# Moving the output projection and the first half of the values within a turn of a pre-norm transformer kernel

## Chip, cores, metric

The kernel runs on one core of one Trainium2 chip. The metric is the device time of one execution in microseconds; less is better. The kernel before takes 3188.39 us (median of 3 runs, 3187.64 to 3191.98).

## What is computed

The input is 16 sequences of 256 tokens of 128 channels, float32. First comes one windowed attention with 16 heads of 8 channels, then six layers, each of an attention and a gated feed-forward. The change lies in the six layers' attention alone:

```python
# x is shifted by one token in half its channels; 16 heads of 64, windows of 32 tokens
q, k, v = split(x @ Wqkv)                  # 128 -> 3 * 1024
q, k = rotary(l2norm(q) * qs), rotary(l2norm(k) * ks)
sim = einsum('bhwie,bhwje->bhwij', q, look(k)) * 8      # own window and the one before
attn = softmax(where(mask, -max, sim))
out = einsum('bhwij,bhwje->bhwie', attn, look(v))
x = out.reshape(b, n, 1024) @ Wo + x
```

## The kernel before

**Tiles and turns.** A layer's 4096 tokens are cut in 32 tiles of 128 tokens. Six layers make 192 tiles, and the main loop (from L904) runs one turn per tile, with a few turns more at the end. A tile passes through several turns: in turn t the kernel projects tile t (`stage_p`), turns round K and Q of tile t-1 and scores it (`stage_s`), takes the exponentials of tile t-2 (`stage_e`), multiplies the probabilities of tile t-3 with its values (`stage_v`), projects the output of tile t-5 (`stage_w`), and does a part of the feed-forward of an earlier pair of sequences (`stage_f`), which is spread over four turns.

**The order inside a turn.** Every stage is a generator. `merge_at` (L248) sorts the steps of all stages by a number between 0 and 1 that the tables of L27 to L29 give them, ties by the order of the stages in the list, and runs them in that order. `mul` and `flip` (L290, L293) pin each TensorE instruction behind the one before, so this order is TensorE's order to the letter. The other engines' orders are made by the framework's scheduler from the same emission; each engine takes its own queue strictly in order, and a PSUM buffer is handed on when its last reader is done.

**The steps of a turn.** These names are used throughout:

- P0 to P5: the six projections of `project` (L626; places c/6): K in two halves, Q in two halves, V in two halves. Each is three matmuls of 128x512 with four 128x128 transposes of `turned` (L610) between them: K halves of tile t-1 in P0 and P1, Q halves in P2 and P3, the probabilities of tile t-2 in P4 and P5. After P0 to P3, DVE multiplies by the rotary table (`mc`, L644), ACT squares (`sq`, L653), DVE reduces the square (`r`, L654), POOL adds the products (`sum`, L655); after the second half of K or Q, ACT takes Ln and Exp of `r` (L659, L660, listed as L275), and POOL clamps `r` (L661) and scales (L665). After P4 and P5, ACT copies `vb` (L671). The transposes are copied by ACT (`kt`, `qt` L622; `pt` L620).
- E: `stage_e`, two matmuls that add the negated maxima to the scores; ACT then takes the two exponentials `p` (L758, listed as L275).
- VA and VB: the first and the second half of `stage_v` (places 0.1 and 0.45). Each is 32 small matmuls into two banks. DVE takes reciprocals and multiplies (`rc` L792, `of` L793), ACT rounds (`ohl` L797), POOL subtracts (`ohl` L798); after VB one DMA transposes `ohl` into `ot` (L801).
- W: `stage_w` (place 0.47), 24 matmuls of `ot` with the output weights; DVE adds the result to the residual (`xg`, L819, two instructions).
- S: `stage_s` (place 0.72), two mask matmuls and 128 small score matmuls; DVE takes the maxima (`nm`, L740).
- Feed-forward, by the turn's number modulo 4: kind 0 centres at 0.86 (FC; ACT squares, L858); kind 1 takes the statistics at 0.06 (ST; ACT Ln and Exp, DVE L864, ACT L867, DVE L868) and two gate projections at 0.74 and 0.88; kind 2 has the third gate projection at 0.03 and two of the other projections at 0.27 and 0.8 (DVE L888); kind 3 the last of these at 0.1 and the second weight matrix at 0.35 (W2; DVE L897, two instructions). The three Gelus on ACT (L281) need their own table, loaded before the first and changed back after the last.

**PSUM.** Eight banks in three pools: two banks for the projections, four shared by transposes, W, VA and the feed-forward, two shared by the scores and VB (`SPLIT`, `USE`, `USE_V`). So VB can start only when the exponentials have read the scores (VB's first bank after the first exponential, the second after the second), and S only when DVE's multiplications `of` have read VB's two banks. W of tile t-5 reads the `ot` that was transposed two turns before.

Of the kernel before, what the change touches and what calls it, by code (L numbers as in the profile page):

```python
# [24 lines left out]
KT = 2  # L25
LAG_S, LAG_P, LAG_V, LAG_W = 1, 2, 3, 5
AT_P = tuple(c / 6 for c in range(6))  # L27
AT_E, AT_V, AT_W, AT_S = (0.2, 0.21), (0.1, 0.45), (0.47,), (0.72,)
AT_F = ((0.86,), (0.06, 0.74, 0.88), (0.03, 0.27, 0.8), (0.1, 0.35, 0.6))  # L29
AT_L = 0.71  # L30
LOAD_AT = 6
# [992 lines left out]
```

## Time and profile before

The profiled execution took 3188.3 us; its span is 3186.5 us, and 1.8 us lie around it. The granted TensorE clock was 0.984 of full speed on average. Busy shares of the span: TensorE matmul 93%, weight load 65%, DVE 80%, ACT 75%, POOL 79%.

The windows view shows where the time lies: 250.0 us to 3140.0 us is the main loop, with 2772.2 us of TensorE, 2349.6 us of DVE, 2167.8 us of ACT and 2355.6 us of POOL busy in 2890 us.

The timeline gives the start of every step on TensorE. This table has the median time from the start of a step to the start of the next, over the 45 or 46 whole turns of each kind. A step takes longer than in other kinds where it, or the first instruction of the next step, waits.

| kind | steps and us from start to start, in TensorE's order | whole turn, median (mean) |
|---|---|---|
| 0 | P0 1.18, VA 0.80, P1 1.09, E 0.43, P2 1.18, VB 1.00, W 1.35, P3 1.08, P4 1.18, S 1.74, P5 1.09, FC 0.86 | 13.06 (13.28) |
| 1 | P0 1.08, ST 0.97, VA 0.79, P1 1.09, E 0.43, P2 1.62, VB 1.26, W 1.35, P3 1.08, P4 1.18, S 1.70, gate 0.66, P5 1.08, gate 0.65 | 14.99 (15.24) |
| 2 | P0 1.45, gate 1.27, VA 1.43, P1 1.09, E 0.43, proj. 0.65, P2 1.45, VB 1.26, W 1.35, P3 1.08, P4 1.18, S 1.74, proj. 0.66, P5 1.08 | 16.14 (16.21) |
| 3 | P0 1.18, VA 1.06, proj. 0.66, P1 1.08, E 0.43, P2 1.08, W2 2.67, VB 0.79, W 1.35, P3 1.08, P4 1.18, S 1.70, P5 1.09 | 15.46 (15.56) |

Four turns are 59.65 us by the medians and 60.29 us by the means. About half of the turns also prepare a piece of the next layer's weights (place 0.71), which adds an instruction or two on ACT and DVE and lengthens the means.

### The profile page before, as it was taken

The numbers are of one execution on the slowest core, as the hardware profiler recorded it, in microseconds if no ns is written. First come the engines' busy times: TensorE is split into PE (matmuls) and PEld (weight loads), VectorE is DVE, ScalarE is ACT, GpSimd is POOL, SyncE is SP. The second block draws the span as 40 slices with busy tenths as digits, with TensorE's granted clock in tenths as the row PEclk, the third lists the DMA queues.
The fourth block names the chain that finished last, engine by engine and source line by source line (L and its number), as shares of the span: only waits on it lengthen the run. The fifth ranks groups of instructions, "written<-read, shape, count | busy, mean of one in ns | idle before, by whom it ended". The sixth has DMA issues, their size and how long they took to land. (4 is left out here: it accounts for less than half of the span.)

```text
span 3186.5 us, 153142 instructions
## 1 busy us (share of the span) xinstructions
PE 2973.4 (93%) x67106; PEld 2081.1 (65%) x67106; DVE 2558.8 (80%) x4690; ACT 2378.3 (75%) x4970; POOL 2525.0 (79%) x2594
## 2 busy tenths in 40 slices
PE   4778999999999999999999999999999999999997
PEld 3555766666666666666666666666666666666664
DVE  6887888888788887788888788888788888878874
ACT  7877777777777777777777777777777777777774
POOL 6767988778888788888788888888888888887882
PEclk9958999999999999999999999999999999999999
DMA  5773444444344434444444444444344444344443
GB/s 118 143 132 81 102 103 94 87 93 88 85 108 100 86 85 94 89 96 103 90 89 82 93 101 99 87 89 92 84 103 106 85 87 96 83 92 106 91 88 72
DMA packets 622942, 302.96 MB, mean 95 GB/s; under 512 B 533446, under 2 KB 545732, under 8 KB 622276
## 3 DMA queue, kind: packets, MB, share of 16 engines
q1 hardware_dynamic: 622276, 293.18, 43.6%
q8 instruction: 528, 8.65, 1.1%
q14 instruction: 138, 1.13, 0.1%
HBM read 22.45 MB, written 4.19 MB: 8 GB/s over the span
## 5 line engine op out<-in xcount | busy, mean ns | idle before, releaser
L291 PE MATMUL bank<-wqkv,xhl 128*128 128x512 f16 x3456 | 1236.6, 381 | 7.7 <-ACT sq L653 6.3
L655 POOL TENSOR_TENSOR sum<-mc 128x512 f32<-128x512 f32 x768 | 994.7, 1298 | 234.1 <-DVE mc L644 223.2
L644 DVE TENSOR_TENSOR mc<-bank,tq 128x1024 f32<-128x1024 f32 x768 | 928.0, 1218 | 147.1 <-PE bank L294 136.3
L665 POOL TENSOR_TENSOR sum<-sum,r 128x512 f32<-128x512 f32 x768 | 795.6, 1057 | 31.9
L654 DVE TENSOR_REDUCE r<-sq 128x8 f32<-128x512 f32 x768 | 520.4, 682 | 276.3 <-ACT sq L653 266.4
L294 PE MATMUL bank<-ident,sum 128*128 128x128 f32 x3072 | 711.3, 273 | 0.7 <-POOL sum L665 0.7
L798 POOL TENSOR_TENSOR ohl<-of,ohl 128x512 f16<-128x512 f32 x384 | 451.1, 1175 | 210.8 <-ACT ohl L797 210.1
L653 ACT ACTIVATE sq<-bank 128x512 f32<-128x512 f32 x768 | 459.4, 608 | 161.8 <-DVE mc L644 160.4
L294 PEld LDWEIGHTS bank<-ident,sum 128*128 128x128 f32 x3072 | 433.1, 141 | 134.2 <-issue 17.5
L291 PEld LDWEIGHTS <-xhl 128*128 128x128 f16 x3456 | 338.0, 98 | 187.4 <-issue 16.7
L797 ACT CAST ohl<-of 128x512 f16<-128x512 f32 x384 | 237.8, 619 | 271.2 <-DVE of L793 268.4
L291 PE MATMUL bank<-vb,pt 64*32 64x65 f32 x6144 | 377.0, 225 | 50.3 <-ACT p L275 26.2
L291 PEld LDWEIGHTS bank<-vb,pt 64*32 64x32 f32 x6144 | 257.4, 105 | 218.5 <-ACT p L275 74.3
L294 PE MATMUL bank<-ident,p 128*128 128x128 f32 x1536 | 354.6, 273 | 0.0
L291 PE MATMUL bank<-v,pt 64*32 64x65 f32 x6144 | 313.5, 224 | 38.5 <-ACT p L275 17.7
L291 PE MATMUL bank<-vw,pt 64*32 64x65 f32 x12288 | 332.4, 225 | 1.8 <-issue 1.5
L793 DVE TENSOR_TENSOR of<-bank,rc 128x256 f32<-128x256 f32 x768 | 295.4, 416 | 1.8
L291 PE MATMUL bank<-ot,wohl 128*128 128x128 f16 x4608 | 291.3, 220 | 0.4 <-DMA ot<-ohl 0.4
L291 PEld LDWEIGHTS bank<-kt,qt 64*32 64x32 f32 x24576 | 256.3, 105 | 44.7 <-issue 44.2
L291 PE MATMUL bank<-kt,qt 64*32 64x64 f32 (+1 forms) x24576 | 284.7, 223 | 0.7 <-issue 0.7
L291 PEld LDWEIGHTS bank<-v,pt 64*32 64x32 f32 x6144 | 235.6, 105 | 70.1 <-ACT p L275 33.1
L291 PEld LDWEIGHTS <-wohl 128*128 128x128 f16 x4608 | 258.9, 98 | 19.1 <-issue 1.3
(155 smaller groups left out, 4965.6 us busy)
## 6 DMA issues: line engine op xcount, KB each, us to landing
v<-vb SPq DMA_DIRECT2D x384, 130.0 KB
vw<-vb SPq DMA_DIRECT2D x384, 130.0 KB
vw<-vb SPq DMA_DIRECT2D x576, 65.0 KB
wraw<-in_L_ffn_Wqkv_dram SPq DMA_DIRECT2D x36, 256.0 KB
wraw<-in_L_ffn_Wo_dram SPq DMA_DIRECT2D x12, 256.0 KB
ot<-ohl SPq DMA_TRANSPOSE x192
xt<-in_L_attn_x_dram SPq DMA_DIRECT2D x8, 256.0 KB
r1d<-xt SPq DMA_DIRECT2D x8, 256.0 KB
```

The lines of the kernel that those rows point to most:

```text
L291: pin(T.matmul(*args, **how))
L294: pin(T.transpose(*args))
L644: V.tensor_tensor(prod, p4.unsqueeze(3).to_broadcast([128, 8, 2, 2, 32]), tq[:, s, d.j].unsqueeze(1).to_broadcast([128, 8, 2, 2, 32]), ALU ...
L653: S.activation(sq, pp.rearrange("p (h d) -> p h d", d=64), AF.Square)
L654: V.tensor_reduce(r[:, hb * 8 : hb * 8 + 8], sq, AX.X, ALU.add)
L655: G.tensor_tensor(mc, m2[:, :, 0], m2[:, :, 1], ALU.add)
L665: G.tensor_tensor(mc, mc, rb.unsqueeze(2).to_broadcast([128, 8, 64]), ALU.mult)
L793: V.tensor_tensor(of[:, :, a], po[a][:, :, 0:64], rc.unsqueeze(2).to_broadcast([128, 4, 64]), ALU.mult)
L797: S.copy(ohl[:, 0, h], of)
L798: G.tensor_tensor(ohl[:, 1, h], of, ohl[:, 0, h], ALU.subtract)
```

## The change

Two numbers of the table of places change:

```diff
-AT_E, AT_V, AT_W, AT_S = (0.2, 0.21), (0.1, 0.45), (0.47,), (0.72,)
+AT_E, AT_V, AT_W, AT_S = (0.2, 0.21), (0.18, 0.47), (0.44,), (0.72,)
```

VA moves from 0.1 to 0.18, and so from behind P0 to behind P1 (P1 stands at 0.167); in kind 3 it also falls behind the feed-forward's projection at 0.1, with which it was tied. W moves from 0.47 to 0.44 and VB from 0.45 to 0.47, so W stands in front of VB. TensorE's order of a turn without feed-forward was P0, VA, P1, E, P2, VB, W, P3, P4, S, P5, and is P0, P1, VA, E, P2, W, VB, P3, P4, S, P5. No instruction is added or removed, and the SP queue keeps its order apart from single transposes that change place with a small load or store.

The other engines' orders follow in the built program. On DVE, kind 0 as an example (the numbers of P in brackets):

```
before: mc(0) rc rc of(VA) r(0) of(VA) mc(1) mc(2) r(1) rc rc r(2) of of(VB) xg xg(W) mc(3) r(3) nm nm
after:  mc(0) mc(1) r(0) rc rc r(1) of of(VA) mc(2) xg xg(W) r(2) rc rc of of(VB) mc(3) r(3) nm nm
```

In each kind `mc(1)` now stands in front of VA's normalization and the two `xg` in front of VB's. On ACT, `kt` of P1 and `sq` of P1 come in front of the exponentials, and behind VB's `ohl` come, as before, `vb` of P4, `pt` of P4 and `sq` of P3, then Ln and Exp, `vb` of P5, `pt` of P5 and, in kind 0, the square of FC. `qt` of P3 stood behind VB's `ohl` in all kinds; it now stands in front of it in kinds 1 and 2.

## The prediction

> **What bounds the kernel now.** I read the page first, then the view of waits, then the timeline engine by engine over four turns without weight pieces: P0 starts at 1241.03 us (kind 3), 1256.14 (kind 0), 1269.12 (kind 1) and 1284.11 (kind 2), and the four turns repeat after 59.21 us.
>
> ```profile
> span 3186.5 us, 153142 instructions
> PE 2973.4 (93%) x67106; PEld 2081.1 (65%) x67106; DVE 2558.8 (80%) x4690; ACT 2378.3 (75%) x4970; POOL 2525.0 (79%) x2594
> ```
>
> TensorE is almost always busy on the page, but a row ends by model, so a wait shorter than the 0.2 us that a small matmul lasts is hidden in it. The table of starts shows more: VB loses 0.10 + 0.21 us in kind 0 (the P2 in front of it takes 1.18 where 1.08 is free, VB 1.00 where 0.79 is), 0.54 + 0.47 in kind 1, 0.37 + 0.47 in kind 2 and nothing in kind 3. That is 2.16 us in four turns. The waits and TensorE's timeline in kind 1 say for what:
>
> ```profile
> ACT ohl L797 <- DVE of L793: 268.4, 238, 2.5
> DVE r L654 <- ACT sq L653: 266.4, 338, 2.2
> ACT r L275 <- DVE r L654: 150.8, 205, 1.9
> PE bank L291 <- ACT p L275: 43.9, 166, 2.9
> ```
>
> ```profile
> 1275.14 0.30 PE L291 MATMUL bank<-vb,pt 64*32 64x65 f32 x2 [0.40 <-ACT p L275]
> 1275.62 0.24 PE L291 MATMUL bank<-v,pt 64*32 64x65 f32 x1 [0.19 <-ACT p L275]
> ```
>
> VB waits for both exponentials. The first three rows show the other loop: ACT stands idle until DVE has normalized (`of`), DVE until ACT has squared, ACT until DVE has reduced. DVE's and ACT's timelines at the end of the turn of kind 0:
>
> ```profile
> 1263.11 0.24 DVE L792 RECIPROCAL rc<-bank 128x4 f32<-128x4 f32 x2
> 1263.28 0.69 DVE L654 TENSOR_REDUCE r<-sq 128x8 f32<-128x512 f32 x1
> 1263.88 0.75 DVE L793 TENSOR_TENSOR of<-bank,rc 128x256 f32<-128x256 f32 x2
> 1264.54 0.58 DVE L819 SCALAR_TENSOR_TENSOR xg<-bank,xg 64x128 f32<-64x128 f32 x2
> 1265.15 1.23 DVE L644 TENSOR_TENSOR mc<-bank,tq 128x1024 f32<-128x1024 f32 x1
> ```
>
> ```profile
> 1264.66 0.62 ACT L797 CAST ohl<-of 128x512 f16<-128x512 f32 x1 [0.82 <-DVE of L793]
> 1265.19 0.58 ACT L622 COPY qt<-bank 128x512 f32<-128x512 f32 x1
> 1265.66 0.59 ACT L671 COPY vb<-bank 128x512 f32<-128x512 f32 x1
> 1266.14 0.60 ACT L620 COPY pt<-bank 128x512 f32<-128x512 f32 x1
> 1266.62 0.62 ACT L653 ACTIVATE sq<-bank 128x512 f32<-128x512 f32 x1
> 1268.05 0.31 ACT L275 ACTIVATE r<-r,tiny 128x16 f32<-128x16 f32 x1 [0.81 <-DVE r L654]
> 1268.39 0.22 ACT L275 ACTIVATE r<-r 128x16 f32<-128x16 f32 x1
> 1268.51 0.57 ACT L671 COPY vb<-bank 128x512 f32<-128x512 f32 x1
> 1268.97 0.59 ACT L620 COPY pt<-bank 128x512 f32<-128x512 f32 x1
> 1269.45 0.61 ACT L858 ACTIVATE gt<-bank 128x512 f32<-128x512 f32 x1
> ```
>
> The reader is to see that DVE goes from row to row without a pause, and that nine ACT instructions stand in file behind VB's `ohl`. The last is FC's square, done at 1270.06; ST, which waits for it, starts on TensorE at 1270.21, directly behind P0 (1.08 after 1269.12). This file has about 0.1 us to spare. In turns with weight pieces it has none: P0 of kind 1 takes 1.31 in the mean against 1.08.
>
> **The change part by part.** Nothing is added or removed, DMAs included; the `ot` that W reads was transposed two turns earlier, so W in front of VB waits for no transfer, and VB's own transpose, later on SP, is read two turns on (some 28 us). Every price below is a row's start to the next start: `mc` 1.13 us (1.22 to its end), `r` 0.60, `rc` 0.08, `of` 0.33, the two `xg` 0.61, an ACT copy or square of 512 columns 0.48 to 0.50 (0.60 to its end), and 1.25 from a P's start to its `mc` (1257.39 after 1256.14).
>
> *W in front of VB: the wait goes.* W's 1.35 us of TensorE lie between P2 and VB and cover 0.31, 1.01 and 0.84: by itself 2.16 us in four turns. The main loop holds 46 such groups, so 99 us. The cover holds although `sq` of P1 now stands in front of the exponentials on ACT: in kind 0 the second exponential ends at 1261.36 instead of 1260.98, and VB starts at 1262.15.
>
> The Trainium skill would stop here: Perfetto Trace Analysis, section Optimization Strategy, has one find the gaps on the most contended engine and make what they wait for start sooner or finish faster. By that rule alone the sum is 3188 less 99, 3089 us; the rows of DVE and ACT speak against it.
>
> *What is late next, kind 0.* DVE has the same work up to `mc(3)`, but the two `xg` now precede VB's normalization. From `mc(1)` at 1258.52: mc, r, 2 rc, r, 2 of, mc, 2 xg, r, 2 rc, 2 of with the pause of 0.2 between `rc` and `of`, end 1265.28 instead of 1264.63: 0.65 later, the two `xg`. `mc(3)` stays (1265.19 for 1265.15). S, at 1265.20, just misses waiting. But `ohl` starts at 1265.32 instead of 1264.66, and the file behind it shifts: `sq(3)` 1267.27 for 1266.62, FC's square to its end 1270.69 for 1270.06, ST 1270.74 for 1270.21. TensorE, 0.07 ahead at P5, now waits 0.6 there: 0.53 lost.
>
> *Kind 1.* ST is 0.53 late, P1 follows it (VA no longer stands between), `mc(1)` at 1272.94. From there DVE has no pause: mc, r, L864 0.62, 2 rc, r, 2 of, mc, L868 0.60, 2 xg, r, 2 rc, 2 of end at 1280.68. VB's 1.01 is won and given back: P4 waits 0.35 for `sq(2)`, S some 0.6 for `of`. S starts, its second mask matmul counted, at 1280.52 instead of 1280.02: still 0.5 late. `sq(3)` is 0.65 late, and with it Ln, Exp, the table load and the three Gelus.
>
> *Kind 2* hangs on those Gelus. VA behind P1 hides part of its 1.26 us of waiting (for `pt` of P5 and the second Gelu), but P2 then waits for `sq(0)` behind the second table load and its transposes for `kt` (0.65 + 0.26). VB's 0.84 is won; DVE, which now waits for `sq(0)` before VA's reciprocals, brings `of(VB)` to 1297.37. S at 1297.20 for 1296.76: 0.44 late, 0.06 won back.
>
> *Kind 3* had no wait at VB, W2 covered it. S comes 12.20 after P0 instead of 12.31, but `of(VB)` ends 0.75 later (1252.88 for 1252.13 on the sample's clock), `sq(3)` 0.64 and `vb` of P5 0.6 later.
>
> *Kind 0 again.* P1 stands directly behind P0 and needs the bank that `vb` of P5 frees: 0.38 of waiting, where VA covered it before. P2 starts 59.91 us after P2 four turns earlier, against 59.21: **0.70 us lost in four turns**.
>
> POOL has the same 12 us a turn; K's scaling comes earlier since `r` of P1 does, so I cost it at nothing. Its cover is 2890 less 2356 us idle, 2.8 us a turn; were that gone, a `sum` of 1.27 would stand in the file.
>
> The skill's page SBUF — State Buffer, section SBUF: two separate sides, says a DVE instruction with two SBUF inputs and a POOL instruction that reads SBUF exclude each other. The trace agrees: the `sum` at 1275.81, beside L868, took 1.65 us against a mean of 1.30. At 0.35 us for each of the 46 L868, 16 us would fall on POOL, whose idle time takes it up.
>
> Sum: 46 times 0.70 is 32 us. Against the profiled execution: 3186.5 + 32 + 1.8 around the span = 3220; its own 3188.3 is the median of 3188.39. **Forecast 3220 us.**
>
> Bounds. Weight pieces add 50 DVE instructions L137 of 0.6 us (ten pieces in each of five layers). I take them at nothing more than before, because most keep their place between VB's `of` and `mc(3)`; all on the path would be 30 us, 3250. The other end is the first rival's.
>
> **The rivals.**
>
> A, faster. ACT's file ends 0.65 later but nobody waits: then kind 0 keeps 0.17 (0.31 less a wait of P2 for `sq(0)`), kind 1 nothing, kind 2 0.40, kind 3 0.10, together 0.67 in four turns, 31 us: 3157. It decides if `of(VB)` is under 0.1 us late in kind 0, as it is if DVE reaches the `xg` before VB's matmuls are done. For it: ACT idles 25% of the span. Against it: DVE's rows show no pause there.
>
> B, no change: waits only move, since DVE sets the pace in both orders (`mc(3)` at the same time in kinds 0 and 1): 3188. For it: those equal times. Against it: ACT's file is longer than DVE's lead.
>
> C, clearly slower: weight pieces lengthen both files, as P0 of kind 1 shows (0.23 in the mean): 3250. Against it: the pieces already cost that before.
>
> **How the numbers follow.** Forecast 0.58 (3197 to 3240), A 0.22, B 0.11, C 0.09. What a measurement tells from no change is 0.2%, 6 us. Faster takes A and a little of B: 0.24; the same most of B: 0.09; slower the rest: 0.67. Range 3152 to 3258: from a little beyond A to a little beyond C.
>
> **What would show it.** Right: no group of VB with `ACT p` as releaser on TensorE; VB's `of` 0.6 or more later against S; new waits of ST for L858, of P1 in kind 0 for `vb`, of P4 for `sq`, of S for `of`; whole turns of kinds 0 and 1 longer by 0.2 to 0.6 each. Wrong: ST starting directly behind P0 in turns without weight pieces, or four turns under 59.2 us.

## The result

The changed kernel takes 3280.38 us (median of 5 runs, 3279.14 to 3283.08) against 3188.14 us before (5 runs beside it, 3185.98 to 3191.98): 1.0289 times as long, 95% interval 1.0275 to 1.0303, or 92 us more. The direction was as forecast, the size not: 32 us were forecast, and the time lies outside the range.

The page of the changed kernel:

```profile
span 3281.3 us, 152963 instructions
PE 2998.9 (91%) x67106; PEld 2075.6 (63%) x67106; DVE 2631.2 (80%) x4690; ACT 2350.1 (72%) x4970; POOL 2525.8 (77%) x2594
```

DVE runs the same 4690 instructions and is busy for 72 us longer (2631.2 against 2558.8). TensorE's busy time rises by 26 us, which I take for waits that fall inside rows of modelled length. So the first question is which DVE instructions became longer. The second is what TensorE now waits for (total us, times, longest):

```profile
ACT ohl L797 <- DVE of L793: 405.3, 190, 3.9
DVE r L654 <- ACT sq L653: 295.5, 370, 1.5
ACT r L275 <- DVE r L654: 143.1, 174, 1.1
PE bank L291 <- DVE of L793: 85.2, 68, 2.1
PE bank L291 <- ACT sq L653: 47.1, 95, 1.5
PE bank L291 <- ACT gt L858: 17.6, 42, 2.6
```

VB's wait for the exponentials (`bank <- ACT p`, 43.9 us in this view before) is down to 0.8 us. In its place S waits for VB's normalization, P4 for the squares `sq`, and ST for FC's square. ACT's idle time in front of `ohl` has grown from 268.4 to 405.3 us.

The steps on TensorE from start to start, medians (where not said otherwise), the main ones that changed:

| kind | changed steps after (before) | whole turn, mean after (before) |
|---|---|---|
| 0 | P0 1.25 (1.18), P2 1.08 (1.18), VB 0.79 (1.00), S 1.94 (1.74) | 13.25 (13.28) |
| 1 | P0 1.56 (1.08), P2 1.08 (1.62), VB 0.79 (1.26), **P3 1.85 (1.08), P4 2.57 (1.18), S 2.03 (1.70)** | 17.24 (15.24) |
| 2 | gate 0.64 (1.27), P1 1.71 (1.09), VA 0.79 (1.43), proj. 1.11 (0.65), VB 0.79 (1.26), P4 1.23 (1.18), in the mean 1.74 (1.17), S 2.06 (1.74) | 16.55 (16.21) |
| 3 | P0 1.08 (1.18), VA 0.79 with P1 in front (1.06) | 15.30 (15.56) |

Four turns take 62.34 us in the mean against 60.29. The 2.05 us times 46 are 94 us, as much as the spans differ by (94.8). Kind 1 alone has lost 2.00 of it.

What became longer on DVE is seen in the groups of instructions (count, then busy us and mean ns of one, then idle time before them). Before:

```profile
L868 DVE TENSOR_TENSOR xnhl<-gt,xnhl 128x512 f16<-128x512 f32 x48 | 32.5, 678 | 0.7 <-ACT xnhl L867 0.7
L864 DVE TENSOR_TENSOR gt<-xg,gt 128x512 f32<-128x512 f32 x48 | 31.9, 665 | 9.6 <-ACT gt L275 9.6
```

After:

```profile
L864 DVE TENSOR_TENSOR gt<-xg,gt 128x512 f32<-128x512 f32 x48 | 65.4, 1363 | 9.0 <-ACT gt L275 9.0
L868 DVE TENSOR_TENSOR xnhl<-gt,xnhl 128x512 f16<-128x512 f32 x48 | 64.7, 1348 | 1.4 <-ACT xnhl L867 1.4
```

The same 96 instructions on the same operands take 130.1 us instead of 64.4. That is 65.7 of DVE's 72 us. The timelines of a turn of kind 1 say why. DVE:

```profile
1365.08 1.23 DVE L644 TENSOR_TENSOR mc<-bank,tq 128x1024 f32<-128x1024 f32 x1 [1.30 <-PE bank L294]
1366.23 0.68 DVE L654 TENSOR_REDUCE r<-sq 128x8 f32<-128x512 f32 x1
1366.82 1.39 DVE L864 TENSOR_TENSOR gt<-xg,gt 128x512 f32<-128x512 f32 x1
...
1370.66 1.38 DVE L868 TENSOR_TENSOR xnhl<-gt,xnhl 128x512 f16<-128x512 f32 x1
1371.96 0.58 DVE L819 SCALAR_TENSOR_TENSOR xg<-bank,xg 64x128 f32<-64x128 f32 x2
```

POOL in the same turn:

```profile
1366.39 1.27 POOL L655 TENSOR_TENSOR sum<-mc 128x512 f32<-128x512 f32 x1 [1.25 <-DVE mc L644]
1370.34 1.15 POOL L798 TENSOR_TENSOR ohl<-of,ohl 128x512 f16<-128x512 f32 x1 [2.67 <-ACT ohl L797]
```

L864 starts 0.43 us after POOL's sum and ends 0.55 us after it (1368.21 for 1367.66). L868 starts 0.32 us after POOL's `ohl` and ends 0.55 after that. So it is in 46 of the 48 norms: each of the two instructions begins while POOL works and ends 0.55 us after POOL's. I read this as standing until POOL is done; the experiments test it. In the kernel before L868 never began beside a running POOL instruction (0 of 48). L864 did in 15 cases, at the very end of one, and took 0.67 us there as elsewhere. The delay reaches TensorE at the end of the chain, where S waits for VB's `of`:

```profile
1373.99 0.72 PE L291 MATMUL bank<-maskb,rowsb 64*128 64x512 bf16 x2 [1.33 <-DVE of L793]
```

### The profile page after: what moved, and what is told of

Same layout as the page of the kernel before. It is cut to its first block, busy times and chain, and to the rows that moved or that the text cites. A ratio compares the mean times of both kernels' runs of the same rounds, so it can differ in the third digit from the quotient of the medians.

```text
span 3281.3 us, 152963 instructions
## 1 busy us (share of the span) xinstructions
PE 2998.9 (91%) x67106; PEld 2075.6 (63%) x67106; DVE 2631.2 (80%) x4690; ACT 2350.1 (72%) x4970; POOL 2525.8 (77%) x2594
## 4 chain that ended last, share of the span: by engine, by line
PE 50%; ACT 20%; DVE 20%; issue 5%; DMA 2%; POOL 2%; SPq 1%; ACTq 0%; POOLq 0%; DVEq 0%
PE bank L291 40%; PE bank L294 9%; DVE r L654 4%; DVE mc L644 4%; DVE of L793 4%; ACT sq L653 3%; ACT vb L671 3%; ACT gt L281 3%; ACT pt L620 2%; DVE xnhl L868 2%; ACT L884 2%; ACT L281 2%; ACT r L275 1%; DMA pt<-ph 1%; DVE rc L792 1%
## 5 line engine op out<-in xcount | busy, mean ns | idle before, releaser
L655 POOL TENSOR_TENSOR sum<-mc 128x512 f32<-128x512 f32 x768 | 987.9, 1289 | 148.8 <-DVE mc L644 142.3
L665 POOL TENSOR_TENSOR sum<-sum,r 128x512 f32<-128x512 f32 x768 | 785.1, 1043 | 28.0
L797 ACT CAST ohl<-of 128x512 f16<-128x512 f32 x384 | 240.6, 627 | 410.8 <-DVE of L793 405.3
L291 PE MATMUL bank<-vb,pt 64*32 64x65 f32 x6144 | 322.8, 224 | 1.3 <-ACT pt L620 1.1
L291 PEld LDWEIGHTS <-wohl 128*128 128x128 f16 x4608 | 273.4, 98 | 43.0 <-issue 29.6
L291 PEld LDWEIGHTS bank<-vb,pt 64*32 64x32 f32 x6144 | 249.2, 105 | 75.0 <-issue 27.9
L291 PE MATMUL bank<-kt,qt 64*32 64x64 f32 (+1 forms) x24576 | 294.6, 225 | 1.7 <-issue 1.5
L793 DVE TENSOR_TENSOR of<-bank,rc 128x256 f32<-128x256 f32 x768 | 287.9, 416 | 1.5
L294 PEld LDWEIGHTS bank<-ident,p 128*128 128x128 f32 x1536 | 216.6, 141 | 86.9 <-issue 37.1
```

The lines of the kernel that those rows point to most:

```text
L291: pin(T.matmul(*args, **how))
L294: pin(T.transpose(*args))
L655: G.tensor_tensor(mc, m2[:, :, 0], m2[:, :, 1], ALU.add)
L665: G.tensor_tensor(mc, mc, rb.unsqueeze(2).to_broadcast([128, 8, 64]), ALU.mult)
L793: V.tensor_tensor(of[:, :, a], po[a][:, :, 0:64], rc.unsqueeze(2).to_broadcast([128, 4, 64]), ALU.mult)
L797: S.copy(ohl[:, 0, h], of)
```

## Experiments

Theory 1: L864 and L868 are delayed by POOL, since `mc` of P1 now comes ahead of L864 and sets off POOL's sum, and the rest of the turn's order falls so that L868 meets POOL's `ohl`. 1.4 us a turn of kind 1 on a DVE that has no pause there, times 46, are 64 of the 92 us. Theory 2, the prediction's own: the two `xg` ahead of VB's normalization make `ohl`, and ACT's file behind it, late. All runs have the same arithmetic as the kernels they come from. The table has the median times, the ratio to the kernel before on the same chip, and the mean turn of each kind.

| run | us | ratio [95% interval] | kinds 0, 1, 2, 3, mean us |
|---|---|---|---|
| changed kernel | 3280.38 | 1.0289 [1.0275, 1.0303] | 13.25, 17.24, 16.55, 15.30 |
| e1, VA alone | 3234.34 | 1.0138 [1.0123, 1.0153] | 13.57, 15.93, 16.34, 15.36 |
| e2, W alone | 3252.01 | 1.0194 [1.0176, 1.0212] | 13.24, 17.56, 15.09, 15.74 |
| e3, norm through PSUM | 3240.00 | 1.0157 [1.0142, 1.0173] | 13.28, 15.87, 16.93, 15.30 |
| e4, the same on before | 3186.94 | 0.9986 [0.9977, 0.9995] | 13.29, 15.25, 16.15, 15.59 |
| g1, norm early on DVE | 3215.85 | 1.0080 [1.0065, 1.0095] | 13.26, 15.65, 16.68, 15.31 |
| g2, `xg` late | 3254.26 | 1.0201 [1.0185, 1.0216] | 13.17, 16.41, 16.81, 15.36 |
| g3, both | 3199.78 | 1.0029 [1.0018, 1.0040] | 13.19, 15.33, 16.62, 15.36 |
| g4, W alone, DVE's order set | 3195.77 | 1.0019 [1.0009, 1.0028] | 13.10, 15.33, 16.16, 15.90 |
| g5, g3 and pieces late | 3200.21 | 1.0031 [1.0019, 1.0043] | 13.26, 15.33, 16.42, 15.53 |
| c1, VA moved in kind 3 only | 3179.75 | 0.9960 [0.9946, 0.9973] | 13.30, 15.17, 16.23, 15.33 |
| c2, c1 and W in kind 0 | 3187.40 | 0.9982 [0.9973, 0.9991] | 13.14, 15.48, 16.23, 15.33 |
| c3, c2 and W in kind 2 | 3181.26 | 0.9964 [0.9951, 0.9976] | 13.17, 15.43, 16.00, 15.47 |

### The two halves of the change alone

```diff
-AT_E, AT_V, AT_W, AT_S = (0.2, 0.21), (0.1, 0.45), (0.47,), (0.72,)
 e1:
+AT_E, AT_V, AT_W, AT_S = (0.2, 0.21), (0.18, 0.45), (0.47,), (0.72,)
 e2:
+AT_E, AT_V, AT_W, AT_S = (0.2, 0.21), (0.1, 0.47), (0.44,), (0.72,)
```

> Only VA behind P1; W stays behind VB, VB where it was. Theory 1 (each of L864 and L868 in kind 1 stands behind a POOL instruction, because mc of P1 now comes ahead of L864): both last about 1.35 us as in the changed kernel, VB's waits for its exponentials stay, and 1.4 us times 46, less what VB's wait of 1.0 us in kind 1 absorbs, come on top: 3215 to 3255. Theory 2 (the two xg ahead of VB's normalization are the cause): they stand behind it here, so 3180 to 3200, however long L864 is.

> Only W in front of VB; VA stays in front of P1. Theory 1: mc of P1 comes behind L864 again, L864 and L868 last 0.67 us each, and what is left of the loss is at most the 32 us of the late ohl: 3170 to 3220. Theory 2: the two xg are ahead of VB's normalization as in the changed kernel, most of the 92 us stay: 3250 to 3285.

With VA moved alone, L864 took 1362 and L868 1354 ns in the mean and the loss was 42 us (1.38%), inside theory 1's range and outside theory 2's. Kind 1 lost 0.69 us of the 1.4 (32 us of the 42), since VB's wait for the exponentials stayed (P2 1.23 and VB 1.27) and takes up a part. Neither theory has the rest: kind 0, which has no norm, lost 0.29, as VB waits longer for the exponentials there (VB 1.29 for 1.00 in the mean), behind the copy and the square of P1 that now precede them on ACT.

With W moved alone, L864 took 668 and L868 682 ns, and yet 60 us (1.94%) were lost, far more than theory 1 left for it: the time lies at the lower end of theory 2's range. Kind 1 is 2.32 us longer, and kind 2 gives 1.12 of it back. DVE in a turn of kind 1 of this run:

```profile
1235.22 1.22 DVE L644 TENSOR_TENSOR mc<-bank,tq 128x1024 f32<-128x1024 f32 x1
1236.35 0.58 DVE L819 SCALAR_TENSOR_TENSOR xg<-bank,xg 64x128 f32<-64x128 f32 x2
1236.97 1.28 DVE L654 TENSOR_REDUCE r<-sq 128x8 f32<-128x512 f32 x2
1238.28 0.25 DVE L792 RECIPROCAL rc<-bank 128x4 f32<-128x4 f32 x2
1238.45 1.19 DVE L644 TENSOR_TENSOR mc<-bank,tq 128x1024 f32<-128x1024 f32 x1
1239.56 0.75 DVE L793 TENSOR_TENSOR of<-bank,rc 128x256 f32<-128x256 f32 x2
```

Here not only the two `xg` but also `mc` of P3 stands ahead of VB's `of`, for which S waits: P4 lasts 2.85 us up to S. So each half loses by itself, and in kind 1 both lose through DVE, in two ways. The run g4 below tests this reading of e2, with both moved at once.

### Taking the collision away through PSUM

```diff
-        xf = gt[:, 1]
-        tab(sq, sq, AF.Exp, scale=-0.5)
+        tab(pm, sq, AF.Exp, scale=-0.5)
+        xf = pm
-            ... src, sq.rearrange(...), ALU.mult
+            ... src, xf.rearrange(...), ALU.mult
```

> The changed kernel, same order, but the layer norm's Exp writes its factor into the PSUM bank that its Ln read, and L864 writes there too, so that L864 and L868 have one SBUF input each. Theory 1: both last 0.6 to 0.8 us although POOL is busy at their start, and some 64 us come back: 3205 to 3230. Theory 2 or a mere coincidence in time with POOL: L864 and L868 short or long, the time stays at 3265 to 3285.

> The control: the kernel before with the same PSUM edit. L864 and L868 were 0.67 us there, so both theories expect nothing: 3182 to 3194. If it is faster by more than 10 us, the edit is worth something by itself and that much is taken off what the run before it shows.

The changed kernel with this edit, DVE in kind 1:

```profile
1351.05 0.69 DVE L864 TENSOR_TENSOR bank<-xg,bank 128x512 f32<-128x512 f32 x1
...
1354.17 0.68 DVE L868 TENSOR_TENSOR xnhl<-bank,xnhl 128x512 f16<-128x512 f32 x1
```

POOL there:

```profile
1350.62 1.27 POOL L655 TENSOR_TENSOR sum<-mc 128x512 f32<-128x512 f32 x1 [1.25 <-DVE mc L644]
```

With one of their two inputs in PSUM, both instructions take 0.68 us in the mean, although POOL is at work when they start in 46 of 48 cases, as in the changed kernel. In L868 nothing but one input changed place, so it is its second SBUF input that made it wait; in L864 the output moved to PSUM too. The control shows the other side: POOL's `sum` that starts 0.16 us behind L868 takes 1.66 us in the kernel before and 1.28 in e4. The time of e3 fell by 40 us, not by the 64 expected, and lies between the ranges of the two theories. On TensorE the edit brings a wait of its own:

```profile
1352.85 1.51 PE L291 MATMUL bank<-ot,wohl 128*128 128x128 f16 x24 [1.12 <-DVE of L793]
```

W, which did not wait in kind 1 of the changed kernel, now stands 1.12 us for VA's normalization: P2 lasts 2.36 us up to W instead of 1.08. I read it as the price of holding ST's bank up to L868 instead of up to Ln, so that W gets one of VA's banks; that was not tested by itself. The control is 0.14% faster than before, as expected within its range, so the edit alone brings 4 to 5 us.

### Setting DVE's order

The next four runs leave operands and TensorE's order alone and fix DVE's order, by an edge to the instruction that is to go first (for the `xg`, W's two adds also become a step of their own, emitted behind VB's). In the changed kernel, the main lines:

```diff
 g1, kind 1: L864 ahead of r of P0's squares, L868 ahead of mc of P2
+                if hb == 0 and s == 1 and ahead:
+                    late_r.append(lambda rb=rb, sq=sq: V.tensor_reduce(rb, sq, AX.X, ALU.add))
...
+        for late in late_r:
+            behind(late(), n864.ins)
 g2, all kinds: xg behind VB's normalization (ofs: VB's last of)
+            behind(made, *ofs)
 g3: both
 g4: W alone (as e2) with the edge of g2, and mc of P3 behind VB's normalization too
```

> The changed kernel, same TensorE order and same banks; only DVE's own order in kind 1 is set: L864 in front of the reduction of P0's squares (so directly behind mc of P1, ahead of POOL's sum of it) and L868 in front of mc of P2 (while POOL is idle). Theory 1 (each stood behind a POOL instruction): both last 0.65 to 0.75 us, POOL's sum about 1.7 instead of 1.27, kind 1 is shorter by 1.2 to 1.4 us a turn, 55 to 64 us in all: 3212 to 3232. If the lock is not what costs time: 3270 to 3290.

> The changed kernel; only the two xg are put behind VB's normalization on DVE, in every turn. L864 and L868 stay behind POOL (1.35 us each). Theory 2 (the two xg make ohl, and ACT's file behind it, late): 28 to 50 us come back, 3230 to 3252. If the lock is the whole loss: 3270 to 3285.

> Both edits of DVE's order at once. If the two causes add and are all there is: 3160 to 3200, about the time before. If something else is left of the 92 us: above 3210. If VB's waits that the change removed are worth what the first rival said: near 3157.

> W in front of VB with VA in front of P1 as before, and DVE's order set so that VB's normalization comes ahead of the two xg and of mc of P3 (in the run with W alone both stood ahead of it in kind 1, and S waited). If that order is what cost W alone its 60 us: 3150 to 3195, and it may beat the kernel before. If W in front of VB loses for another reason: 3230 to 3255.

g1 in kind 1, DVE and then POOL:

```profile
1224.12 0.68 DVE L871 TENSOR_TENSOR gt<-xg,gt 128x512 f32<-128x512 f32 x1
...
1226.70 0.68 DVE L879 TENSOR_TENSOR xnhl<-gt,xnhl 128x512 f16<-128x512 f32 x1
```

```profile
1224.28 1.65 POOL L662 TENSOR_TENSOR sum<-mc 128x512 f32<-128x512 f32 x1 [1.25 <-DVE mc L645]
```

(L871 and L879 are L864 and L868, L662 is L655.) The pair of the changed kernel is turned round. The norm's multiply starts 0.16 us ahead of POOL's sum and takes 0.68 us; now the sum is long, 1.65 us for 1.27. POOL can afford it. 64.5 us come back, as much as theory 1 expected at most, and kind 1 falls from 17.24 to 15.65 us.

g2 brings 26 us, a little less than the lower end of what was expected. Kind 1 and, by 0.08, kind 0 are shorter, kind 2 is longer by 0.26. ST still waits for FC's square (P0 of kind 1 1.55), so the two `xg` were not what made that square late; the account of the prediction below shows what did.

g3 has both, stands at the upper end of what was expected, and is 81 us faster than the changed kernel: of the 91 that the two bring alone, 10 are not there together. It is 0.29% slower than before. g4, W alone with VB's normalization first, is 56 us faster than e2 and confirms the reading of e2 (the two moves together; their shares were not parted). But it does not beat the kernel before either, and lies just above what was expected.

### The weight pieces

What was left in g3, some 9 us, lies in kind 2 (16.62 for 16.21). In 20 of its 46 turns P4 lasts 2.38 us up to S in the mean (2.44 in the changed kernel, 1.18 in the same turns before); the other 26 turns are no longer than before. DVE in such a turn of the changed kernel:

```profile
453.11 0.25 DVE L792 RECIPROCAL rc<-bank 128x4 f32<-128x4 f32 x2
453.28 1.06 DVE L137 SCALAR_TENSOR_TENSOR wqkv<-wraw,wqkv 128x512 f16<-128x512 f32 x1
454.26 0.74 DVE L793 TENSOR_TENSOR of<-bank,rc 128x256 f32<-128x256 f32 x2
```

A piece of the next layer's weights stands between VB's reciprocal and its `of`.

```diff
 g5: g3, and in the pieces' second half (L137)
+        behind(made, *ofs)
```

> The run with both edits of DVE's order, and as a third the weight pieces' second half (L137) put behind VB's normalization. In the changed kernel P4 of kind 2 takes 2.44 us up to S in 20 of 46 turns, where a piece stands between rc and of of VB, and 1.20 in the others; such turns are 1.0 us longer (1.2 with both edits). If that is what was left of the loss: 20 to 24 us less than the run with both edits, 3174 to 3182, just under the kernel before. If the piece only moves to another place on the path: 3195 to 3205.

The long P4 of such turns went away in ten of the 20 (1.18 for 2.13 us in the turn that starts at about 438 us), and the mean of P4 in kind 2 fell from 1.69 to 1.48. But the time stayed: kind 2 is 0.20 shorter, kind 3 0.17 and kind 0 0.07 longer. The other ten come from pieces that g5 left where they were: once a layer 3.22 us behind two multiplies of 1.1 us for `tq`, and once a layer 2.02 us behind a scaling of `w2t` of 1.0 us (L181 and L224 of the kernel before). So what g5 reached moved and was not won, and what the last 9 us hang on was not settled.

### A version that keeps one part

```diff
 c1: the kernel before, and
-            (LAG_V, AT_V, stage_v),
+            (LAG_V, (0.18, 0.45) if t % 4 == 3 else AT_V, stage_v),
 c2, c3: also W in front of VB in kind 0 (c3: 0 and 2), with the edges of g4
```

> The kernel before with VA behind P1 in turns of kind 3 alone, where no feed-forward norm runs and where the changed kernel was 0.26 us shorter. If the gain belongs to that turn alone: 0.2 to 0.26 us times 46, 9 to 12 us less than before, 3176 to 3183. If the next turn gives it back: within 4 us of before.

> As the last one, and W in front of VB in turns of kind 0 alone, with VB's normalization ahead of the two xg and of mc of P3 on DVE. If what W wins there (0.18 us in the run with W alone and this order) is kept: 8 us more, 3168 to 3176. If ST of kind 1, which waits for FC's square, gives it back: no change against the last one, 3176 to 3184.

> As the last one, and the same in turns of kind 2. If the 0.84 us of wait in front of VB there can be kept: up to 35 us less, down to 3135. If ACT's Gelus set that turn's pace, as the run with W alone and this order shows (16.16 for 16.21 us): within 5 us of the last one.

c1 is 0.40% faster than before (0.27 to 0.54%) and so beats both kernels; c3, with more moved, is no better. Turns of kind 3 have no L864 and no L868 that could collide, and they are 0.23 us shorter. c2 is slower than c1 and above both ranges expected of it: in c2 kind 0 gains 0.16 us and kind 1 gives back 0.31 (P0 1.51 for 1.25, the wait of ST for FC's square). c3 wins 6 us of that again: kind 2 gains 0.23 of the 0.84 that VB waited there, and kind 3 gives 0.14 back.

## Why the prediction was right and wrong

**The wait goes: right.** VB starts without waiting in all kinds (0.79 us each), and the 2.16 us in four turns are won at that place. In kind 2, P2 stays at 1.46 us all the same: its transposes now wait for `kt`, as the prediction has it.

**It is given back by DVE and ACT: right, and more completely than the forecast's own terms say.** g3 and g4 have no wait at VB, no long L864 and no `xg` ahead of `of`, and still take 0.2 to 0.3% more than before. 99 us were won at one step and lost at others. ACT's file at the end of kind 0 shows the exchange:

```profile
1357.41 0.62 ACT L797 CAST ohl<-of 128x512 f16<-128x512 f32 x1 [1.75 <-DVE of L793]
...
1361.27 0.57 ACT L671 COPY vb<-bank 128x512 f32<-128x512 f32 x1
1361.73 0.59 ACT L620 COPY pt<-bank 128x512 f32<-128x512 f32 x1
1362.21 0.61 ACT L858 ACTIVATE gt<-bank 128x512 f32<-128x512 f32 x1
```

From `ohl` to the end of FC's square it takes 5.41 us, as in the prediction's turn (1264.66 to 1270.06). But in the median turn of kind 0 `ohl` starts 9.25 us after P0 instead of 8.52, while S starts 9.26 after P0 instead of 9.34. So ST, behind P0 from 1361.32, starts only at 1362.88. P0 of kind 1 is 0.48 us longer by the medians (0.53 was predicted), 0.24 by the means, since the weight pieces had filled a part of it before.

The prediction laid the late `ohl` to the two `xg`: 0.65 us. That 0.73 was measured is near it by luck, for with the `xg` out of the way (g2) `ohl` still starts 9.01 after P0, and ST waits as long. DVE in a turn of kind 0 of g2:

```profile
1219.03 1.22 DVE L644 TENSOR_TENSOR mc<-bank,tq 128x1024 f32<-128x1024 f32 x1
1220.91 0.69 DVE L654 TENSOR_REDUCE r<-sq 128x8 f32<-128x512 f32 x1 [0.66 <-ACT sq L653]
1221.51 0.24 DVE L792 RECIPROCAL rc<-bank 128x4 f32<-128x4 f32 x2
1221.72 0.76 DVE L793 TENSOR_TENSOR of<-bank,rc 128x256 f32<-128x256 f32 x2
```

`mc` of P2 now comes behind VA's normalization. ACT's square of P2 follows it, and DVE stands 0.66 us for that square before the reduction and VB's `rc` and `of` behind it. In the changed kernel the two `xg` (0.61 us) fill most of this pause (0.17 is left). The prediction has no pause for that square here.

**The 32 us: near in size, not in place.** With the collision taken out (g1) the change costs 26 us (3215.85 against 3189.60 before), where 32 were forecast. Setting the `xg` late brought 26 in g2 and 16 on top of g1 (3215.85 to 3199.78). But in g2 the gain lies in kind 1 (16.41 for 17.24), where S waits for VB's `of`; kind 0 is only 0.08 shorter, and ST's wait, through which the prediction led the loss from turn to turn, stayed.

**The step that failed: the shared port.** The prediction priced it with "At 0.35 us for each of the 46 L868, 16 us would fall on POOL, whose idle time takes it up", and kind 1's chain with "L864 0.62" and "L868 0.60". The row it relied on (a sum of 1.65 us beside L868) is right, and g1 shows the same 1.65. But it is no cost of the change, since the sums beside L868 take 1.66 us in the kernel before already, and it shows only who gives way when DVE is first. The change itself turned the order round, `mc` of P1 and POOL's sum before L864, and the prediction had written that new order down without asking who would then be first. Each L864 and L868 cost 1.31 us from start to next start instead of 0.62 and 0.60, on the engine without a pause: 1.4 us a turn, and 64 of the 92 us came back when g1 took it out.

The Trainium skill, SBUF — State Buffer, section SBUF: two separate sides, says that the one that starts first has the port pair for its whole instruction and the other fully blocks. The two orders of the same pair agree with it: 0.68 beside 1.65 us with DVE first, 1.39 beside 1.27 with POOL first. The page limits this to DVE instructions with two SBUF inputs, or in a mode that uses both ports; e3 agrees (0.68 us beside a running POOL with one input in PSUM).

**By kinds.** From P0 to P0 the prediction's terms give kind 0 +0.31, kind 1 +0.57, kind 2 -0.06 and kind 3 -0.11 us. Measured were -0.03, +2.00, +0.34 and -0.26. Kind 1 is off by the 1.4 of the collision. The prices listed for kind 0 add up to 1265.12 for the end of `of`, with one pause of 0.2, and not to the 1265.28 written; that is small beside it. In kind 0 the wait of P1 for `vb` of P5, put at 0.38, lengthened P0 by only 0.04 in the mean.

**The bound for the weight pieces: wrong.** They were taken "at nothing more than before, because most keep their place between VB's `of` and `mc(3)`". In 20 turns of kind 2 a piece stood ahead of `of`; in ten of them it was `tq` or `w2t`, which the prediction did not count. The mean of the main loop's 50 L137 rose from 763 to 910 ns: L137 reads two SBUF operands too, and in the changed kernel it took 1.01 us in the mean where it began beside POOL (35 cases) and 0.68 where it did not. Such turns were 1.0 us longer than the other turns of kind 2, about 20 us before what later turns win back. As g5 shows, that sum can't simply be added, and the pieces' own share of the 92 us was not measured.

**The rivals.** A (faster) fell with DVE's rows, as argued against it. B (waits only move) is what is left when the collision and the `xg` are taken out. C (clearly slower) was nearest in size, but not through its own mechanism, longer files by the weight pieces: most of the loss came back in g1, which left the pieces as they were.

## What to carry to other kernels

When a reordering brings a POOL instruction's trigger ahead of a DVE instruction that reads two SBUF operands, ask which of the two now starts first. The one that is second pays most of what is left of the first, and if it is on the engine without pauses the price is the kernel's. A wait removed on TensorE is worth only what the engines behind it can follow: here two orders that removed all of it (g3, g4) were no faster than before, while a smaller move, in turns of kind 3 alone (c1), was, by 0.4%.

## What was not expected of the hardware

The blocked instruction shows as long, not as waiting. It costs either engine most of what is left of the other's instruction: L864 was 0.71 us longer with 0.84 of POOL's `sum` left, the `sum` 0.38 longer with 0.52 of L864 left (g1). L864 and L868 alike end 0.55 us after POOL. The same two instructions beside the same POOL work take 0.68 us with one operand in PSUM.

The granted clock says little here. In the ten runs of the kernel before beside g5 it lay between 0.958 and 0.997, and the times do not follow it: 3191.96 us at 0.997, 3191.36 at 0.959, 3188.54 at 0.997 and 3188.61 at 0.976.
